# A fused graph-attention, feed-forward and expert kernel: dense sums from PSUM, nine result buffers, shorter first and last dispatches, three pairs a period over the last sixteen batches

## The chip, the cores and the metric

The kernel runs on one core of one Trainium2 chip. The metric is the device time of one execution in microseconds (us), the lower the better. A profile records one execution: its span runs from the first to the last instruction, and its own time lies a little above the span.

## The reference

Two layers follow one another on x, 64 batches of 256 nodes with 256 features, all in float32:

```python
x = x + gnn0(layernorm(x), adj)          # 4 heads of 64: leaky scores, masked softmax over nodes, elu
x = x + layernorm(x) @ ffn_w.T + ffn_b   # 256 -> 256
x = x + gnn1(layernorm(x), adj)          # 1 head of 256: leaky scores, masked softmax, relu
x = x + moe(layernorm(x))                # see below
```

In moe each of the 16,384 nodes is a token. The router gives 8 logits; the two largest, through a softmax over the two, are the token's weights. With e running over the 8 experts:

```python
h = gelu(tokens @ w1[e] + b1[e])
y = h @ w2[e] + b2[e]
out = tokens + sum over e of combine[:, e] * y      # combine is zero but for two experts
```

## The kernel before

**Batches.** One pass per batch of 256 nodes (two tiles of 128 rows) does both attention layers and the feed-forward layer: `batch_layers`. PE makes projections (L384, L419), scores (L454, L438) and attention sums (L475), DVE the masked scores z (L461, L443) and the statistics of the norms (L353, L354), ACT exponentials and copies out of PSUM, POOL the inverse deviations rstd (L361, L362). The normed result goes into a tile xng, its sum with the residual into `base`, which is stored to the output. Then PE makes the router logits into a tile lg.

**Routing and dispatch.** The first 62 batches are grouped in chunks: twelve of four batches, six of two, two of one. When a chunk is full, `route` finds each token's two experts and the place of each copy in a region per expert in DRAM, the buffer xs. POOL then sends the rows there with an indirect DMA (`send`, L877): two sends for each of the chunk's tiles of 128 rows, 248 in all.

**Pairs.** 256 rows of one expert's region are a pair; there are 131, of which 14 are a flush at the end, filled up with spare rows. `expert_pair` loads the pair's rows (xr, four DMAs of 64 KB, and xt, their numbers and weights) and the expert's first matrix (we, 288 KB) through SP, turns xr on DVE into sT (L116), makes the hidden layer on PE (ph, L783) and ACT (gelu, L789), the second product on PE (py, L798), adds the bias on DVE into a buffer y (L804), and scales y by the weights on ACT (L776). `scatter` then has POOL add y's rows to the output in DRAM with two indirect DMAs (L815). Because two pairs may hold rows of one token, each pair's scatters wait until those of the pair before have landed. The y buffers are a ring of `YBUFS` = 7; one is free again when its scatters have landed.

**Dense batches.** The last two batches are not routed. For each of them and each of 8 experts `dense_expert` uses the same `hidden` and `result`, and two DVE operations (L843) add w * y to `base`. So 16 of the 147 uses of y are dense ones.

**The order of the work.** One loop at the end of the kernel emits everything. Each job is a generator; in every step each active job advances to its next `yield`, in the order of the rank that it yielded last (a negative rank: once more in the same step). [...] Three steps are a period; the loop begins at step 2. A batch begins in every period at phase 2 (batch b at step 2 + 3b; batch 63 at 191, after which `more` becomes false). At phase 1 waiting pairs begin while there is `credit`: two are added each period, three when no batch is left to begin. At phase 2 up to two dense experts begin. One scatter begins in each step if one is waiting. A pair takes these steps, counted from its beginning: 0 loads of xr and xt; 1 load of we; 2 the turn (rank 95); 4 hidden; 5 result (rank 80); 6 scaling; its scatter from 7 on. `later(rank, phases)` makes a job wait for a phase; a chunk's sends go out two at a time, in two of the three phases.

Following the counters of this loop: the first pair begins at step 49, the eight of the second chunk at steps 61 to 70; the last pair at step 232; the last scatter is emitted at step 241.

Of the kernel before, what the change touches and what calls it, by code (L numbers as in the profile page):

```python
# [9 lines left out]
F32 = mybir.dt.float32  # L10
I32 = mybir.dt.int32
AF = mybir.ActivationFunctionType
ALU = mybir.AluOpType
AX = mybir.AxisListType

P = 128
# [11 lines left out]
def kernel(  # L28
# [17 lines left out]
    nc = tc.nc  # L46
    B, N, D = x.shape
    E = router.shape[0]
# [3 lines left out]
    NT = N // P  # L52
# [16 lines left out]
    ROW = D + 4  # L69
    TICKS = 3  # L70
# [3 lines left out]
    work = ctx.enter_context(tc.tile_pool(name="work", bufs=2))  # L74
    small = ctx.enter_context(tc.tile_pool(name="small", bufs=4))
# [171 lines left out]


    C_B1, WROW = KT * D, KT * D + 64
    WBUFS, XBUFS, YBUFS = 7, 5, 7  # L250
    wpack = tc.dram_tile([E, P, WROW], F32, name="wpack")
    w2s = const.tile([P, E, KT * D], F32, tag="w2s", name="w2s")
    b2s = const.tile([P, E, D], F32, tag="b2s", name="b2s")
# [158 lines left out]
    def projected1(xT, rstd, b):  # L412

        q = q1s[b % 2]
        pqs = []
        for t in range(NT):
            pq = bank("pq", [D + 3])
            for k in range(KT):
                nc.tensor.matmul(  # L419
                    pq, xT[:, k, t * P : (t + 1) * P], wx1[:, k, :],  # L420
                    start=(k == 0), stop=(k == KT - 1),
                )
            pqs.append(pq)
        ex = small.tile([P, NT, 3], F32, tag="ex1", name="ex1")
        for t, pq in enumerate(pqs):
            nc.scalar.activation(ex[:, t, :], pq[:, D:], AF.Exp, scale=rstd[:, t : t + 1])
            nc.scalar.activation(
                q[:, t, :D], pq[:, :D], AF.Copy, scale=rstd[:, t : t + 1]
            )
        me = work.tile([P, NT, N], F32, tag="me", name="me")  # L430
        for j in range(NT):
            nc.scalar.activation(me[:, j, :], masks[1][:, j, :], AF.Copy, scale=ex[:, j, 0:1])
        return q, ex, me
# [274 lines left out]
    GROUP = 8  # L708

    def expert_pair(j, n, ids, ef, regs, needs):  # L710

        i = j % GROUP
        upto = min(j + GROUP, n)
        if i == 0:
            _, regs["e"] = nc.values_load_multi_w_load_instructions(
                ids[0:1, 0, j:upto], engines=[mybir.EngineType.SP], min_val=0, max_val=E - 1,
                skip_runtime_bounds_check_because=WHY,
            )
            _, regs["t"] = nc.values_load_multi_w_load_instructions(
                ids[0:1, 1, j:upto], engines=[mybir.EngineType.SP], min_val=0, max_val=E * CAP,  # L720
                skip_runtime_bounds_check_because=WHY,
            )
        e_sp, t_sp = regs["e"][i], regs["t"][i]
        xr = io.tile([P, PAIR // S, KT * S], F32, tag="xr", name="xr", bufs=XBUFS)
        loads = [
            nc.sync.dma_start(
                out=xr[g * S : (g + 1) * S],
                in_=xs_d.rearrange("(t c q) f -> t q c f", c=PAIR // S, q=S)[
                    bass.ds(t_sp, 1), :, :, g * KT * S : (g + 1) * KT * S
                ].rearrange("t q c f -> (t q) c f"),  # L730
            )
            for g in range(P // S)
        ]

        xt = small.tile([P, 2, ROW - D], F32, tag="xt", name="xt", bufs=12)
        loads.append(
            nc.sync.dma_start(
                out=xt,
                in_=xs_d.rearrange("(t k p) c -> t p k c", p=P, k=2)[
                    bass.ds(t_sp, 1), :, :, D:  # L740
                ].rearrange("t p k c -> (t p) k c"),
            )
        )
        for load in loads:
            tc.add_to_no_dep_group("rows", load.ins)
            for name in needs:
                tc.add_manual_dep(
                    load.ins, name, AFTER, reason="any sent row may lie in the pair"
                )
        yield 90  # L750
        we = io.tile([P, WROW], F32, tag="we", name="we", bufs=WBUFS)
        nc.sync.dma_start(
            out=we, in_=wpack[bass.ds(e_sp, 1), :, :].rearrange("e p c -> (e p) c")
        )
        yield 95
        xT = turned(work.tile([P, KT, PAIR], F32, tag="sT", name="sT", bufs=3), xr)
        w = small.tile([P, 2], F32, tag="w", name="w", bufs=8)
        yield 30
        yield 30
        hT = hidden(xT, we)  # L760
        yield -65
        nc.vector.scalar_tensor_tensor(
            w[:, :, None], xt[:, :, 1:2], ef[:, j : j + 1], xt[:, :, 2:3],
            op0=ALU.is_equal, op1=ALU.mult,
        )
        nc.vector.tensor_tensor(w[:, :, None], w[:, :, None], xt[:, :, 3:4], ALU.add)
        yield 80
        if i == 0:
            _, regs["x"] = nc.values_load_multi_w_load_instructions(
                ids[0:1, 0, j:upto], engines=[mybir.EngineType.PE, mybir.EngineType.DVE],  # L770
                min_val=0, max_val=E - 1, skip_runtime_bounds_check_because=WHY,
            )
        y = result(hT, bass.ds(regs["x"][i], 1))
        yield 2
        for t in range(2):
            nc.scalar.activation(y[:, t, :], y[:, t, :], AF.Copy, scale=w[:, t : t + 1])  # L776
        scatters.append((y, xt))
# [13 lines left out]
            )  # L791
        return hT

    def result(hT, e):
        py = bank("py", [2, D])
        for t in range(2):
            for f in range(KT):
                nc.tensor.matmul(  # L798
                    py[:, t, :], hT[:, f, t * P : (t + 1) * P],
                    w2s[:, e, f * D : (f + 1) * D].rearrange("p e c -> p (e c)"),  # L800
                    start=(f == 0), stop=(f == KT - 1),
                )
        y = io.tile([P, 2, D], F32, tag="y", name="y", bufs=YBUFS)
        nc.vector.tensor_add(y, py, b2s[:, e, :].to_broadcast([P, 2, D]))  # L804
        return y
# [25 lines left out]
    def dense_expert(b, e):  # L831

        own = dense_batch[b]
        yield 90
        we = io.tile([P, WROW], F32, tag="we", name="we", bufs=WBUFS)
        nc.sync.dma_start(out=we, in_=wpack[e])
        yield 40
        yield 30
        hT = hidden(own["xT"], we)
        yield 80  # L840
        y = result(hT, slice(e, e + 1))
        for t in range(NT):
            nc.vector.scalar_tensor_tensor(  # L843
                own["base"][:, t, :], y[:, t, :], own["w"][:, t, e : e + 1],
                own["base"][:, t, :], op0=ALU.mult, op1=ALU.add,
            )
        if e == E - 1:
            while b == B - 1 and (scatters or len(added) < 2 * PAIRS):
                yield 99
            d = nc.sync.dma_start(  # L850
                out=out_rows[b * N : (b + 1) * N, :].rearrange("(t p) d -> p t d", p=P),
                in_=own["base"],
            )
            before = added[-2:] + based if b == B - 1 else []
            tc.declare_no_dep(
                d.ins, query=SYNC, group="out", keep=before,
                reason="no row is added to here, or every add is in their chain",
            )
            for ins in before:
                tc.add_manual_dep(d.ins, ins.name, AFTER, reason="filling rows were added here")  # L860
            tc.add_to_no_dep_group("out", d.ins)
            nc.sync.nop()
# [10 lines left out]
    order, order_steps = [], []  # L873
# [14 lines left out]
    def later(rank, *phases):  # L888

        yield rank  # L890
        while order_steps[-1] % TICKS not in phases:
            yield rank

    def route(c, row0, nt, n, last, xng, lg):
# [59 lines left out]
        for t in range(nt):  # L954
            for k in range(2):
                send(xng[t // NT][:, t % NT, :], pos[:, k, t : t + 1])
            if n and spread and t in (1, 3):
                ids, ef = next(parts) or (None, None)
            if not last:
                yield from later(95, 1, 2)  # L960
            elif t % 2:
                yield 95
# [53 lines left out]
    def jobs():  # L1016
        b = done = taken = 0
        for c, nb in enumerate(CHUNKS + (1,) * DENSE):
            nt = nb * NT
            lg = keep.tile([P, nt, E], F32, tag="lg", name=f"lg_{c}", bufs=10)  # L1020
            xng = []
            row0 = b * N
            done += nt
# [13 lines left out]

    batches = jobs()
    step, more, credit = 2, True, 0.0
    SETUP_AT = 3  # L1040
    with tc.manual_schedule():
        while more or active or waiting or dense_jobs or scatters:
# [6 lines left out]
            if step >= SETUP_AT and setup:  # L1049
                begin(setup.pop(0)(), 90)  # L1050
            if phase == 1:
                credit = min(credit + (2.0 if more else 3.0), 3.0)
                while waiting and credit >= 1.0:
                    credit -= 1.0
                    begin(waiting.pop(0)(), 90)
# [58 lines left out]
```

## Time and profile before

| | |
|---|---|
| median of three runs | 1666.84 us (1666.26 to 1670.07) |
| profiled execution, its own time | 1670.08 us |
| its span | 1668.3 us |
| mean granted TensorE clock | 0.958 |
| PE busy | 1495.5 us, 90% |
| DVE busy | 1317.4 us, 79% |
| ACT busy | 833.2 us, 50% |
| POOL busy | 889.4 us, 53% |
| scatters L815 | 262, mean 1591 ns of issue |
| sends L877 | 248, mean 1012 ns of issue |
| sums y, L804 | 147, mean 688 ns |
| multiply-adds into base, L843 | 32, mean 482 ns |
| from the last scatter's issue to the end of the span | 10.0 us |

PE is TensorE's matmuls, DVE VectorE, ACT ScalarE, POOL GpSimd, SP the engine that issues most DMAs. A group or a wait is named by line, engine and tile (out<-in). In a wait the left side is who waited and the right side whom it waited for, with the total, the number of times and the longest. The timeline gives the start, the duration, the engine, the line, the operation and, in brackets, how long the engine sat idle before it and what ended that. The number behind xN in a merged row counts instructions; one matmul of the program on float32 is two in the trace.

### The profile page before, as it was taken

How to read it: one execution, taken by the hardware profiler on the slowest of the kernel's cores; microseconds unless marked ns; L12 is line 12 of the kernel's file. 1: busy time of each engine (PE TensorE's matmuls, PEld its weight loads, DVE VectorE, ACT ScalarE, POOL GpSimd, SP SyncE). 2: the span in 40 equal slices, each digit the busy share in tenths (PEclk: the TensorE clock that was granted, in tenths of full speed). 3: DMA queues.
4: the chain of work that ended last, by engine and by line, in shares of the span. 5: the costliest groups of instructions: out<-in, count | busy, mean ns of one | idle time of the engine just before them, and what ended most of it. 6: DMA issues, size and time to landing. Idle time of an engine off the chain costs nothing.

```text
span 1668.3 us, 30242 instructions
## 1 busy us (share of the span) xinstructions
PE 1495.5 (90%) x8474; PEld 1311.2 (79%) x8474; DVE 1317.4 (79%) x4478; ACT 833.2 (50%) x1832; POOL 889.4 (53%) x853
## 2 busy tenths in 40 slices
PE   5898888899999999999999999999989987678782
PEld 4777777688888888888888888888878876567671
DVE  6888989999898988898989898998889876423330
ACT  0243444455656666666666665655555565323221
POOL 0121433545757575757575757574764666444344
PEclk8999999999999999999999999999999998879986
DMA  3812223255757575756575766665564676866753
GB/s 107 231 41 58 61 70 94 74 142 114 167 118 163 118 159 129 140 132 146 133 149 134 145 133 146 137 140 121 123 142 99 115 156 141 200 135 112 155 107 44
DMA packets 365285, 209.74 MB, mean 126 GB/s; under 512 B 264376, under 2 KB 335040, under 8 KB 365120
## 3 DMA queue, kind: packets, MB, share of 16 engines
q1 hardware_dynamic: 314496, 139.43, 34.0%
q0 software_dynamic: 49632, 67.39, 22.5%
q8 instruction: 70, 1.15, 0.3%
q10 hardware_dynamic: 992, 0.99, 0.2%
q14 instruction: 95, 0.78, 0.2%
HBM read 118.55 MB, written 89.15 MB: 124 GB/s over the span
## 4 chain that ended last, share of the span: by engine, by line
PE 55%; DVE 26%; DMA 6%; issue 5%; POOL 4%; ACT 2%; SPq 1%; DVEq 0%; POOLq 0%; ACTq 0%
PE ph L783 14%; PE pv L475 12%; PE py L798 9%; PE pq L384 5%; PE pq L419 4%; DVE z L461 4%; PE pf L529 4%; DVE stats L353 4%; DMA out_dram<-y,xt 3%; PE pt L368 3%; POOL out_dram L815 2%; DVE mv L354 2%; PE pl L599 2%; PE pd L454 1%; DVE x L535 1%
## 5 line engine op out<-in xcount | busy, mean ns | idle before, releaser
L815 POOL DMA_INDIRECT out_dram<-y,xt x262 | 416.7, 1591 | 255.4 <-DMA out_dram<-y,xt 73.0
L475 PE MATMUL pv<-q,z 128*128 128x65 f32 (+1 forms) x2560 | 369.8, 299 | 6.7 <-DVE z L461 5.3
L475 PEld LDWEIGHTS pv<-q,z 128*128 128x128 f32 x2560 | 331.9, 194 | 19.5 <-DVE z L461 5.8
L783 PE MATMUL ph<-sT,we 128*128 128x256 f32 x1048 | 259.1, 405 | 56.2 <-DVE sT L116 47.1
L361 POOL TENSOR_SCALAR rstd<-mv 128x4 f32<-128x4 f32 (+1 forms) x132 | 69.7, 528 | 436.1 <-DVE mv L354 352.9
L877 POOL DMA_INDIRECT xs<-xng,pos x248 | 251.1, 1012 | 69.2 <-issue 66.9
L783 PEld LDWEIGHTS ph<-sT,we 128*128 128x128 f32 x1048 | 209.8, 205 | 90.9 <-DVE sT L116 50.6
L798 PE MATMUL py<-w2s,hT 128*128 (+1 forms) x1176 | 263.9, 379 | 1.4 <-DVE z L461 0.7
L798 PEld LDWEIGHTS py<-w2s,hT 128*128 128x128 f32 x1176 | 219.7, 190 | 29.7 <-DVE z L461 1.0
L374 ACT COPY xT<-pt 128x512 f32<-128x512 f32 x192 | 113.3, 590 | 222.4 <-PE pt L368 184.7
L804 DVE TENSOR_TENSOR y<-py,b2s 128x512 f32<-128x512 f32 x147 | 97.5, 688 | 158.9 <-PE py L798 88.7
L789 ACT ACTIVATE hT<-ph,we 128x256 f32<-128x256 f32 x294 | 122.8, 471 | 183.3 <-PE ph L783 80.9
L461 DVE SCALAR_TENSOR_TENSOR z<-pd,q,mask 128x256 f32<-128x256 f32 x512 | 211.1, 473 | 0.3 <-PE pd L454 0.2
L362 POOL TENSOR_TENSOR rstd<-rstd,mhalf 128x4 f32<-128x4 f32 (+1 forms) x132 | 162.6, 1232 | 11.0
L776 ACT ACTIVATE y<-y,w 128x256 f32<-128x256 f32 x262 | 113.1, 501 | 104.4 <-DVE y L804 96.3
L353 DVE BATCH_NORM_STATS2 stats<-x 128x6 f32<-128x256 f32 x384 | 156.3, 407 | 2.2
L384 PE MATMUL pq<-wx,xT 128*128 128x268 f32 x512 | 137.9, 415 | 8.6 <-DVE wt L257 4.2
L419 PE MATMUL pq<-wx,xT 128*128 128x259 f32 x512 | 129.1, 394 | 15.5 <-ACT xT L374 11.2
L529 PE MATMUL pf<-wfT,xT 128*128 128x256 f32 x512 | 125.0, 388 | 0.0
L419 PEld LDWEIGHTS pq<-wx,xT 128*128 128x128 f32 x512 | 91.9, 189 | 41.9 <-ACT xT L374 22.4
L384 PEld LDWEIGHTS pq<-wx,xT 128*128 128x128 f32 x512 | 100.9, 202 | 30.1 <-issue 6.9
L551 ACT ACTIVATE rel<-pv,rinv 128x256 f32<-128x256 f32 x128 | 54.0, 474 | 108.2 <-DVE rinv L482 95.8
(151 smaller groups left out, 2233.8 us busy)
## 6 DMA issues: line engine op xcount, KB each, us to landing
we<-wpack SPq DMA_DIRECT2D x147, 288.0 KB
xr<-xs SPq DMA_DIRECT2D x524, 64.0 KB
xblk<-in_x_dram SPq DMA_DIRECT2D x256, 64.0 KB
xin<-in_x_dram SPq DMA_DIRECT2D x64, 256.0 KB
out_dram<-base SPq DMA_DIRECT2D x64, 256.0 KB
out_dram<-y,xt POOLq DMA_INDIRECT x262
xs<-xng,pos POOLq DMA_INDIRECT x248
xs<-fill SPq DMA_DIRECT2D x9, 260.0 KB
```

What stands on the lines that cost most here:

```text
L353: nc.vector.bn_stats(stats[:, t, :], src[:, t, :])
L362: nc.gpsimd.tensor_tensor(rstd[:, :n], rstd[:, :n], mhalf[:, :n], ALU.pow)
L384: nc.tensor.matmul(pq.rearrange("p h c -> p (h c)"), xT[:, k, t * P : (t + 1) * P], wx[:, k, :], start=(k == 0), stop=(k == KT - 1),)
L419: nc.tensor.matmul(pq, xT[:, k, t * P : (t + 1) * P], wx1[:, k, :], start=(k == 0), stop=(k == KT - 1),)
L461: nc.vector.scalar_tensor_tensor(z[:, j, :], pd[:, i, :], q[:, j, h, d + 2 : d + 3], mask[:, j, :], op0=ALU.max, op1=ALU.mult,)
L475: nc.tensor.matmul(pv[:, h, :], z[:, j, t * P : (t + 1) * P], q[:, j, h, : d + 1], start=(j == 0), stop=(j == NT - 1),)
L529: nc.tensor.matmul(pf[:, t, :], xT[:, k, t * P : (t + 1) * P], wfT[:, k, :], start=(k == 0), stop=(k == KT - 1),)
L783: nc.tensor.matmul(ph[:, f, :], we[:, k * D + f * P : k * D + (f + 1) * P], xT[:, k, :], start=(k == 0), stop=(k == KT - 1),)
L789: nc.scalar.activation(hT[:, f, :], ph[:, f, :], AF.Gelu, bias=we[:, C_B1 + f : C_B1 + f + 1])
L798: nc.tensor.matmul(py[:, t, :], hT[:, f, t * P : (t + 1) * P], w2s[:, e, f * D : (f + 1) * D].rearrange("p e c -> p (e c)"), start=(f == 0 ...
L815: d = nc.gpsimd.indirect_dma_start(out=out_rows, out_offset=bass.IndirectOffsetOnAxis(ap=xt[:, t, 0:1].bitcast(I32), axis=0), in_=y[:, t, ...
L877: d = nc.gpsimd.indirect_dma_start(out=xs_d[: E * CAP * PAIR, :], out_offset=bass.IndirectOffsetOnAxis(ap=at, axis=0), in_=xe, in_offset=None,
```

## The change

1. `WBUFS, XBUFS, YBUFS = 7, 5, 9`: the ring of y has nine buffers.
2. Dense experts no longer take a y. The product stays in PSUM, and four DVE operations per expert add w * py and w * b2 to `base`.
3. While the last sixteen batches are begun (from step 3 * 48 = 144 on), three pairs may begin in a period instead of two.
4. The first two chunks send four times in each step, in consecutive steps. Once no batch is left to begin, no job waits for a phase in `later`.
5. Once no batch is left to begin, a pair's turn is emitted at rank 75, that is ahead of the sums of the same step, instead of 95.
6. The dense batch's store is emitted one step later, with rank 99.
7. Buffers: me 2 to 1, xt 12 to 14, w 8 to 12, lg 10 to 7. The lists of expert numbers for PE and DVE are loaded once per group of eight under a key of the group, with unchanged contents and number of loads.

By the same counters, after the change the first pair begins at step 40, the eight of the second chunk at 52 to 61, the last pair at 229, and the last scatter is emitted at step 237. Pairs begun per period at steps 145, 148, 151, 154: three, two, two, one before; three, three, two, none after, and so on in each cycle of four batches up to step 178. At steps 184, 187, 190 and 193 three begin instead of two.

```diff
-    WBUFS, XBUFS, YBUFS = 7, 5, 7
+    WBUFS, XBUFS, YBUFS = 7, 5, 9
...
-        me = work.tile([P, NT, N], F32, tag="me", name="me")
+        me = work.tile([P, NT, N], F32, tag="me", name="me", bufs=1)
...
-        xt = small.tile([P, 2, ROW - D], F32, tag="xt", name="xt", bufs=12)
+        xt = small.tile([P, 2, ROW - D], F32, tag="xt", name="xt", bufs=14)
...
-        yield 95
+
+        yield 95 if more else 75
         xT = turned(work.tile([P, KT, PAIR], F32, tag="sT", name="sT", bufs=3), xr)
-        w = small.tile([P, 2], F32, tag="w", name="w", bufs=8)
+        w = small.tile([P, 2], F32, tag="w", name="w", bufs=12)
...
-    def result(hT, e):
+    def product(hT, e):
         py = bank("py", [2, D])
...
+        return py
+
+    def result(hT, e):
+        py = product(hT, e)
         y = io.tile([P, 2, D], F32, tag="y", name="y", bufs=YBUFS)
         nc.vector.tensor_add(y, py, b2s[:, e, :].to_broadcast([P, 2, D]))
         return y
...
-        y = result(hT, slice(e, e + 1))
-        for t in range(NT):
-            nc.vector.scalar_tensor_tensor(
-                own["base"][:, t, :], y[:, t, :], own["w"][:, t, e : e + 1],
-                own["base"][:, t, :], op0=ALU.mult, op1=ALU.add,
-            )
+        py = product(hT, slice(e, e + 1))
+        for t in range(NT):
+            for add in (py[:, t, :], b2s[:, e, :]):
+                nc.vector.scalar_tensor_tensor(
+                    own["base"][:, t, :], add, own["w"][:, t, e : e + 1],
+                    own["base"][:, t, :], op0=ALU.mult, op1=ALU.add,
+                )
         if e == E - 1:
+            yield 99
...
         yield rank
-        while order_steps[-1] % TICKS not in phases:
+        while more and order_steps[-1] % TICKS not in phases:
             yield rank
...
-            if not last:
+            if c < 2:
+                if t % 2:
+                    yield 95
+            elif not last:
                 yield from later(95, 1, 2)
...
-            lg = keep.tile([P, nt, E], F32, tag="lg", name=f"lg_{c}", bufs=10)
+            lg = keep.tile([P, nt, E], F32, tag="lg", name=f"lg_{c}", bufs=7)
...
+    DRAIN_AT = TICKS * (B - 16)
...
-                credit = min(credit + (2.0 if more else 3.0), 3.0)
+                credit = min(credit + (2.0 if step < DRAIN_AT else 3.0), 3.0)
```

More of the change, by code (lines that the diff above doesn't have):

```diff
@@ L712, in expert_pair @@
         i = j % GROUP
-        upto = min(j + GROUP, n)
+        upto = min(j - i + GROUP, n)
         if i == 0:
@@ L767, in expert_pair @@
         yield 80
-        if i == 0:
-            _, regs["x"] = nc.values_load_multi_w_load_instructions(
-                ids[0:1, 0, j:upto], engines=[mybir.EngineType.PE, mybir.EngineType.DVE],
+        if ("x", j - i) not in regs:
+            _, regs["x", j - i] = nc.values_load_multi_w_load_instructions(
+                ids[0:1, 0, j - i : upto], engines=[mybir.EngineType.PE, mybir.EngineType.DVE],
                 min_val=0, max_val=E - 1, skip_runtime_bounds_check_because=WHY,
             )
-        y = result(hT, bass.ds(regs["x"][i], 1))
+        y = result(hT, bass.ds(regs["x", j - i][i], 1))
         yield 2
```

## The prediction

> **What bounds the kernel now.** I read the slices first, to find stages with different limits, then busy time by stretch, then the waits and the timeline of the stage that looked unbound. Slices (page, part 2; each digit is a tenth of a 41.7 us slice):
>
> ```profile
> PE   5898888899999999999999999999989987678782
> DVE  6888989999898988898989898998889876423330
> POOL 0121433545757575757575757574764666444344
> DMA  3812223255757575756575766665564676866753
> ```
>
> PE is full up to about slice 31; then everything drops and nothing is full. Busy time by stretch says how full:
>
> ```profile
> core 0: us, PE busy (x) PEld busy (x) DVE busy (x) ACT busy (x) POOL busy (x), PEclk, DMA share, GB/s
> 778.00:864.00 86.00, 85.05 (x511) 76.14 (x510) 77.26 (x257) 52.74 (x113) 56.06 (x53) 1.00 0.66 141
> 1223.00:1293.00 70.00, 68.16 (x385) 60.53 (x385) 63.74 (x232) 40.35 (x87) 36.08 (x36) 0.95 0.51 111
> 1347.00:1410.00 63.00, 48.73 (x221) 41.81 (x220) 46.14 (x228) 32.64 (x69) 42.91 (x41) 0.88 0.73 153
> 1460.00:1557.00 97.00, 74.75 (x320) 63.66 (x320) 31.74 (x74) 27.67 (x64) 41.91 (x28) 0.90 0.68 133
> 1557.00:1636.00 79.00, 70.28 (x288) 59.31 (x288) 27.52 (x66) 25.09 (x58) 34.94 (x23) 0.90 0.62 111
> ```
>
> First row: four batches with eight pairs in steady state, PE 99% busy. The last batch is begun at 1293 us (its transpose of xblk). From 1460 the batches are gone; pairs, dense experts and scatters remain, and PE is busy 77%. What holds that stage, from the waits of 1460 to 1636 (us in total, times, longest):
>
> ```profile
> PE ph L783 <- DVE sT L116: 39.6, 8, 9.8
> DVE y L804 <- DMA out_dram<-y,xt: 19.4, 6, 6.2
> ```
>
> and one period of it in the timeline (start, us, engine, what, idle before and its releaser):
>
> ```profile
> 1480.13 0.69 DVE L804 TENSOR_TENSOR y<-py,b2s 128x512 f32<-128x512 f32 x1 [3.20 <-DMA out_dram<-y,xt]
> 1480.85 1.54 POOL L815 DMA_INDIRECT out_dram<-y,xt  x1 [3.79 <-DMA out_dram<-y,xt]
> 1486.65 0.69 DVE L804 TENSOR_TENSOR y<-py,b2s 128x512 f32<-128x512 f32 x1 [5.83 <-DMA out_dram<-y,xt]
> ...
> 1489.69 1.89 DVE L116 STREAM_TRANSPOSE sT<-xr 128x512 f32<-128x512 f32 x3
> 1490.45 2.07 PE L783 MATMUL ph<-sT,we 128*128 128x256 f32 x4 [9.07 <-DVE sT L116]
> ```
>
> All seven y buffers are out; the sum at L804 waits for a scatter to land; the three transposes of the next pairs stand behind it on DVE; PE waits for them. Last, the end, nothing but scatters:
>
> ```profile
> 1651.90 1.54 POOL L815 DMA_INDIRECT out_dram<-y,xt  x1 [2.97 <-DMA out_dram<-y,xt]
> 1653.75 1.54 POOL L815 DMA_INDIRECT out_dram<-y,xt  x1 [0.30 <-issue]
> 1658.29 1.54 POOL L815 DMA_INDIRECT out_dram<-y,xt  x1 [2.99 <-DMA out_dram<-y,xt]
> ```
>
> One pair's two scatters must land before the next pair's are issued: 6.4 us a pair here, with nothing else running. So there are two bounds: PE while batches run, the scatter chain at the end, and between them a loop that couples the two.
>
> [...] The chain of waits has 3.67 to 3.70 us from issue to landing at the end, of which 1.54 is the issue: 2.1 left[...].
>
> **The change, part by part.** Steps are those of the emitting loop, followed by hand through its counters; a batch enters every 3 steps (a period), a steady period is 21.45 us (85.8 for four), a step 7.15.
>
> (a) Three pairs a period from step 144. The queue of waiting pairs is fed two per batch. Up to step 180 it is empty at the end of each cycle of four batches before and after, so pairs only move inside a cycle: 3, 2, 2, 1 begun per period becomes 3, 3, 2, 0. From step 181 there is backlog: at 184, 187, 190 and 193 three are begun instead of two. From 194 both begin three. So four pairs go from the drain into periods that still hold batches. With the last dispatches (below) the last scatter is emitted at step 237 instead of 241.
>  Gain: four scatters fewer in the chain at the end. In the drain the spacings that the chain alone sets run from 6.4 to 7.2 us, about 6.9: 4 x 6.9 = -28.
>  Cost 1: a pair is 8 matmuls at L783 and 8 at L798, 222 ns apart in the drain (40 in 8.9 us): 16 x 0.222 = 3.55 us of PE. Steps 184 to 197 are PE-full (68.2 of 70): 4 x 3.55 = +14. If PE's later holes (14 us in 1347 to 1410) absorb it, 0.
>  Cost 2: a period with no pair holds 21.45 - 7.1 = 14.35 us of PE work, but DVE needs (77.3/4) - 2 x 1.75 = 15.8 there, and batches without pairs took 18 (277 to 350: 73 for four). So 1.4 to 3.7 us lost a cycle in PE-full time, three or four cycles: +4 to +14; +6 taken.
>
> (b) Nine y buffers, none for dense experts, and the turn at rank 75 once no batch is left to begin. Five y a period came from seven buffers; now three from nine. The turns stand ahead of the sums on DVE, so PE no longer waits 2.4 to 9.8 us a period. If xr came late, the sums and the scatters would now stand behind it; but in the drain before it is issued 14 to 41 us ahead of its turn, and SP's place in the order is not touched. [...] PE needs 5 experts x 3.55 = 17.7 us a period, the chain 3 x 6.9 = 20.7. The chain becomes the bound, against about 22 now (turns at 1490, 1512, 1532, 1557, 1579, 1600, 1623): 1.3 us x 8 periods = -10. Ends: 0 if the chain itself slows with more traffic, -20 if it runs at 6.4.
>
> (c) Dense sums from PSUM. Removed 16 sums of 688 ns, added 32 multiply-adds. [...] the trace shows 464 to 473 ns with a PSUM source (L535, L461) and 482 without (L843), so 0.48 us each: 32 x 0.48 - 16 x 0.69 = +4.3 us of DVE, 0.5 a period, under DVE's 70% idle time. 0; without that cover +4. The PSUM bank is held 1.9 us instead of 0.7; PE comes round to it half a period later.
>
> (d) First dispatches: chunks 0 and 1 issue four sends a step for four steps, instead of two in two steps of three; their nine pairs come nine steps sooner, but chunk 2's stay, so PE work is only swapped between two cycles: 0. POOL has 4 x 1.28 = 5.1 us of sends a step plus 1.33 norms x 1.76 = 2.3, in steps of 6: rstd may come late. 8 steps x 1.4 = +11 at worst; POOL waits for DVE's mv up to 10 us there, which hides most: +2. Nothing below 0 unless PE's 10 us of holes in 277 to 350 are used, -5.
>
> (e) Last dispatches: no waiting for phases once batches are out; the last send is at step 206 instead of 208, in (a)'s four steps. One buffer of me: written once a period, read a step later: 0. lg in 7, xt in 14, w in 12, the register lists, the dense store one step later (it now stands behind the loads on SP): 0; if SP's place matters, a few us either way.
>
> Sum: -28 + 14 + 6 - 10 + 0 + 2 = -16 on the span of 1668.3 (its run 1670.08): 1652. The median of the runs is 1666.84, so I forecast 1650 to 1651.
>
> **Rivals.**
>  *Absorbed* (0.22): PE's later holes take the four pairs, so cost 1 falls away, and the chain runs near 6.6: -28 - 16 + 6 + 2 = -36, 1631. For: 14 us of PE idle in 1347 to 1410, 16 in 1410 to 1460. Against: PE is 97% full just before.
>  *Chain slows* (0.15): the drain's DMA share is 0.62 to 0.83; with the same bytes in less time scatters land later, spacing 7.3, (b) gains nothing: -29 + 14 + 6 + 2 = -7, 1660. This is the change not doing what it says.
>  *POOL takes over* (0.13), slower: scatters now come one a step in runs of eight and, from step 188, without end, while batches still need rstd. POOL then has 3.7 (scatter) + 1.7 (sends) + 2.3 (norms) = 7.7 us a step against 7.15, and a scatter that waits for the one before holds rstd behind it: the trace has ACT L392 waiting 80 us for rstd in all. Against: POOL is 65% busy in steady state and the four steps without scatters catch up 3 us each. If not caught up, eight steps x 0.55 = 4.4 a cycle x 4, plus 15 steps x 0.8 = 30: +14, 1681. It decides from about 16 us of stretch over steps 152 to 203, 0.3 a step.
>
> **How the numbers follow.** Forecast 0.50, span of cases 1640 to 1660. The unknown costs (cost 1 from 0, cost 2 to 14, (b) from 0 to -20, (d) to 11) and the rivals reach from 1626 to beyond 1680; 1628 to 1667 leaves out the slow rival and some of the best case. A measurement here tells about 0.3% (5 us) from no change: faster is all of the forecast and of *absorbed* and half of *chain slows*, 0.80; same 0.08; slower 0.12.
>
> **What would show it.** Waits of y for out_dram and of ph for sT gone in the drain; scatters 6.6 to 7 us apart there without the 8 to 9 us hole per group of three; turns of the last pairs about 15 us earlier; steady stretches unchanged (86 us for four batches), the last batch's first transpose some 10 us later than 1293, since PE is fuller. Wrong if the holes remain, if scatters spread, or if ACT's waits for rstd grow between 1000 and 1400.

## The result and the profile after

The change makes the kernel slower: 1684.19 us in the median of five runs (1676.36 to 1687.07) against 1666.84; the ratio is 1.0101, with a 95% interval of 1.0081 to 1.0121. The forecast was 1650, and its range ended at 1667. The profiled execution has a span of 1684.0 us.

The slices of the page after the change, answering to the four shown of the kernel before:

```profile
PE   5898888899899999999999999898999997599840
DVE  5888988898998989898989898888988877544320
POOL 0121526157447575657575756467574677433444
DMA  3812223455456575656665665647474666896633
```

After a hole in slices 34 and 35, PE is now nearly full in 36 to 38, which are the drain, but the span is 16 us longer (a slice is 42.1 us here). Busy time by stretch after the change (same columns as before: start and end, length, PE, PEld, DVE, ACT and POOL busy with counts, PE clock, DMA share, GB/s):

```profile
778.00:864.00 86.00, 85.05 (x513) 76.15 (x511) 77.11 (x255) 52.62 (x113) 55.35 (x54) 1.00 0.65 140
1316.00:1374.00 58.00, 56.85 (x327) 50.66 (x327) 49.92 (x188) 36.75 (x80) 42.04 (x38) 1.00 0.65 132
1471.00:1540.00 69.00, 69.00 (x319) 60.66 (x319) 29.81 (x66) 27.69 (x63) 27.84 (x18) 0.99 0.82 171
1540.00:1610.00 70.00, 60.67 (x266) 51.67 (x264) 25.10 (x62) 19.95 (x50) 28.20 (x19) 0.95 0.61 120
```

The steady state is as it was. In the first part of the drain (1471 to 1540) PE is busy 69.0 of 69 us, so the stall that the prediction showed is gone. Waits of the drain, 1471 to 1622:

```profile
DVE y L809 <- DMA out_dram<-y,xt: 54.2, 10, 9.6
...
POOL out_dram L820 <- DMA out_dram<-y,xt: 33.8, 9, 7.1
```

No wait of ph for sT is left, but y waits for scatters longer than before (54.2 us against 19.4), with nine buffers instead of seven. The results that PE now gives sooner stand in a longer queue. The timeline shows the queue's head:

```profile
1525.93 1.54 POOL L820 DMA_INDIRECT out_dram<-y,xt  x1 [0.30 <-ACT hT L790]
...
1533.68 1.54 POOL L820 DMA_INDIRECT out_dram<-y,xt  x1 [6.21 <-DMA xr<-xs]
1535.53 1.54 POOL L820 DMA_INDIRECT out_dram<-y,xt  x1 [0.30 <-issue]
...
1539.47 0.69 DVE L809 TENSOR_TENSOR y<-py,b2s 128x512 f32<-128x512 f32 x1 [5.29 <-DMA out_dram<-y,xt]
1540.19 1.54 POOL L820 DMA_INDIRECT out_dram<-y,xt  x1 [3.12 <-DMA out_dram<-y,xt]
```

POOL sat idle 6.2 us between two pairs and 3.1 us between the next two, while y's stood ready (the last scaling of the y that is added at 1533.68 ended at 1485.0): the scatters are one chain, in which each pair waits for the landing of the one before.

Where the time went is read by laying the two traces side by side at equal steps of the emitting loop. Batch b's first transpose marks step 2 + 3b; later steps are marked by the scatters in their order (start of a pair's first scatter at L815 before, L820 after):

| point | before, us | after, us | after minus before |
|---|---|---|---|
| batch 12 | 205.0 | 208.0 | +3.0 |
| batch 16 | 277.0 | 285.3 | +8.3 |
| batch 24, first dispatches done | 434.5 | 446.3 | +11.8 |
| batch 48, three a period begins | 949.6 | 961.1 | +11.5 |
| batch 60, step 182 | 1222.8 | 1245.0 | +22.2 |
| scatter of step 191 | 1301 | 1325 | +24 |
| scatter of step 203 | 1379 (the 93rd pair's) | 1422 (the 97th pair's) | +43, four pairs ahead |
| last scatter | 1658 (step 241) | 1674 (step 237) | +16 |

So there are three losses of 12, 12 and 19 us and one gain of 27. These are single executions: at batch 8, ahead of any send, the traces of all runs below lie between 132.9 and 139.1 us, so a microsecond or two in the first rows says little.

### The profile page after: what moved, and what is told of

It reads as the page before. It is cut to its first block, busy times and chain, and to the rows that moved or that the text cites. A ratio compares the mean times of both kernels' runs of the same rounds, so it can differ in the third digit from the quotient of the medians.

```text
span 1684.0 us, 30247 instructions
## 1 busy us (share of the span) xinstructions
PE 1496.0 (89%) x8474; PEld 1313.9 (78%) x8474; DVE 1323.9 (79%) x4494; ACT 821.6 (49%) x1826; POOL 887.4 (53%) x853
## 4 chain that ended last, share of the span: by engine, by line
PE 59%; DVE 16%; DMA 9%; POOL 6%; issue 4%; ACT 4%; SPq 2%; POOLq 0%; DVEq 0%; ACTq 0%
PE pv L475 14%; PE ph L784 12%; PE py L799 11%; PE pq L384 6%; DMA out_dram<-y,xt 5%; PE pq L419 5%; PE pf L529 4%; PE pt L368 3%; POOL out_dram L820 3%; DVE z L461 3%; DVE stats L353 2%; PE pl L599 2%; ACT xT L374 2%; POOL xs L884 1%; SPq L726 1%
## 5 line engine op out<-in xcount | busy, mean ns | idle before, releaser
L820 POOL DMA_INDIRECT out_dram<-y,xt x262 | 416.0, 1588 | 256.6 <-DMA out_dram<-y,xt 78.6
L799 PE MATMUL py<-w2s,hT 128*128 (+1 forms) x1176 | 267.7, 384 | 9.9 <-DVE base L849 6.4
L784 PE MATMUL ph<-sT,we 128*128 128x256 f32 x1048 | 242.5, 387 | 11.3 <-DMA we<-wpack 9.1
L784 PEld LDWEIGHTS ph<-sT,we 128*128 128x128 f32 x1048 | 200.6, 195 | 39.0 <-issue 9.8
L809 DVE TENSOR_TENSOR y<-py,b2s 128x512 f32<-128x512 f32 x131 | 85.9, 686 | 92.7 <-DMA out_dram<-y,xt 57.9
L384 PE MATMUL pq<-wx,xT 128*128 128x268 f32 x512 | 144.5, 430 | 8.6 <-DVE wt L257 4.2
L384 PEld LDWEIGHTS pq<-wx,xT 128*128 128x128 f32 x512 | 104.5, 209 | 32.0 <-issue 7.2
L419 PEld LDWEIGHTS pq<-wx,xT 128*128 128x128 f32 x512 | 92.0, 190 | 42.3 <-ACT xT L374 31.0
L354 DVE BATCH_NORM_AGGREGATE mv<-stats 128x2 f32<-128x6 f32 x512 | 93.2, 182 | 17.5
```

The source lines that it names most:

```text
L384: nc.tensor.matmul(pq.rearrange("p h c -> p (h c)"), xT[:, k, t * P : (t + 1) * P], wx[:, k, :], start=(k == 0), stop=(k == KT - 1),)
L419: nc.tensor.matmul(pq, xT[:, k, t * P : (t + 1) * P], wx1[:, k, :], start=(k == 0), stop=(k == KT - 1),)
L784: nc.tensor.matmul(ph[:, f, :], we[:, k * D + f * P : k * D + (f + 1) * P], xT[:, k, :], start=(k == 0), stop=(k == KT - 1),)
L799: nc.tensor.matmul(py[:, t, :], hT[:, f, t * P : (t + 1) * P], w2s[:, e, f * D : (f + 1) * D].rearrange("p e c -> p (e c)"), start=(f == 0 ...
L820: d = nc.gpsimd.indirect_dma_start(out=out_rows, out_offset=bass.IndirectOffsetOnAxis(ap=xt[:, t, 0:1].bitcast(I32), axis=0), in_=y[:, t, ...
```

## The experiments

Theory A is what this table suggests: each loss belongs to the part of the change that acts at these steps. Theory B puts the loss into the drain. In the expectations, "the second kernel" and "the third kernel" are those of the second and third experiments; the third is the base of most later ones. Runs are compared through their ratios to the kernel before, run beside them on the same chip; 0.1% is 1.7 us. Intervals in brackets are of 95%.

**1. First sends put back.**

```diff
-            if c < 2:
-                if t % 2:
-                    yield 95
-            elif not last:
+            if not last:
```

> The changed kernel with the first two chunks' sends put back to two in two of three steps; all else as changed. Theory A (read from the two traces at equal steps: the changed kernel is 12 us behind once chunk 1's pairs are done, another 12 after steps 144 to 180, another 19 after steps 191 to 203, and then gains 27 by four scatters fewer): 12 us under the changed kernel, about 1672. Theory B (the loss comes from scatters that follow one another in every step of the drain and from the dense sums, and early differences are absorbed later): within 3 us of the changed kernel, 1681 to 1687.

1671.88 us, ratio 1.0010 (0.9999 to 1.0020).

**2. Three a period only from step 180.**

```diff
-    DRAIN_AT = TICKS * (B - 16)
+    DRAIN_AT = TICKS * (B - 4)
```

> The changed kernel with three pairs a period only from step 180 on, so that steps 144 to 179 begin 3, 2, 2, 1 pairs a period as before, while the four pairs of steps 184 to 193 are still drawn ahead. Theory A: the 12 us of steps 144 to 180 come back, about 1672. Theory B: within 3 us of the changed kernel. The prediction's own term for this part was 6 us, with 4 to 14 as its ends.

1669.99 us, ratio 0.9996 (0.9985 to 1.0008).

**3. Both of these edits.**

> Both of the two edits above together: what is left of the change is nine y buffers, dense sums from PSUM, the turn ahead of the sums, four pairs drawn ahead and the shorter last dispatches. Theory A: 1684 - 24 = 1660, about 7 us under the kernel before (0.4% faster). Theory B: above 1675.

1657.67 us, ratio 0.9925 (0.9911 to 0.9938): faster than both kernels.

**4. The first edit, and the pace of before.**

```diff
-                credit = min(credit + (2.0 if step < DRAIN_AT else 3.0), 3.0)
+                credit = min(credit + (2.0 if more else 3.0), 3.0)
```

> The changed kernel with the first sends back and the pace of pairs as before (two a period while batches are left to begin, then three): only buffers, dense sums, the turn's place, the store's place and the last dispatches are changed. Theory A: the scatter chain was already the bound of the drain before, at about 7.3 us a pair with loads running, and PE freed from waiting gives nothing: 1664 to 1670, no difference from before. The prediction's term for this part was -10: 1657. Theory B: above 1672.

1674.39 us, ratio 1.0028 (1.0013 to 1.0044).

The four close the account. In per cent of the time before: the first dispatches cost 0.71 to 0.91 (runs 2 and 3; changed kernel and run 1), 12 to 15 us. The pattern of steps 144 to 179 costs 0.85 to 1.05, 14 to 17 us. The four pairs drawn ahead gain 1.03 (runs 4 and 3), 17 us. What is left, buffers, dense sums, the turn's place and last dispatches, is +0.28, 5 us (2 to 7). Theory B is refuted: from the 97th pair's first scatter to the last pair's, run 3 takes 250.5 us and the changed kernel 252.0, and run 3 is the fastest so far. The +0.28 of run 4 was not expected; its profiled execution (span 1667.4), one of its fastest, shows no such loss, so it stays unexplained. Run 4 has all of (b), the prediction's central part, and TensorE waits for no sT in its drain, yet it is not faster than the kernel before.

**5 and 6. What sets the pace of the drain.** Run 5 leaves out the dense experts' work but keeps their loads; run 6 leaves out the loads too.

```diff
         we = io.tile([P, WROW], F32, tag="we", name="we", bufs=WBUFS)    # run 6: without these
         nc.sync.dma_start(out=we, in_=wpack[e])                          # two lines
...
-        hT = hidden(own["xT"], we)
         yield 80
-        py = product(hT, slice(e, e + 1))
-        for t in range(NT):
...
```

> The third kernel (both edits back) with the dense experts' hidden layer, product and sums left out, so that the last two batches miss their experts; their weight loads (288 KB each, two a period) stay. It takes 7.2 us of TensorE work out of each period of the drain and no transfer. Theory A (the chain of scatters sets the drain, and its pace is set by the loads beside it, not by waits for y): the spacing of scatters in the drain stays at 7.2 to 7.5 us a pair, the end moves by less than 5 us. Rival (the long gap once per group of three is a wait for the results, as the prediction read it): the gaps shrink, spacing 6.9 or less, the end 12 us earlier or more.

> As the run before, with the dense experts' weight loads left out as well: 0.58 of about 2 MB of loads a period are gone. Theory A: scatters land sooner, spacing 6.5 to 6.9 us a pair over some 24 pairs, the end 10 to 20 us earlier than with the loads. Rival: no difference from the run before.

1661.53 us, ratio 0.9957 (0.9943 to 0.9972), and 1652.41, 0.9899 (0.9882 to 0.9916). From the 103rd pair's scatter to the 121st's, the spacing in the traces is 7.69 us in run 3 (1446 to 1585), 7.70 in run 5 and 7.19 in run 6 (1447 to 1577); over the last ten pairs it is 6.4 in all three. Run 5 has 42 us less PE work than run 3 in this stretch and the same spacing of scatters; taking away transfers shortens it. Busy time of run 5, then of run 3:

```profile
1446.00:1585.00 139.00, 89.54 (x348) 72.69 (x347) 34.98 (x92) 35.35 (x85) 55.74 (x37) 0.83 0.72 148
```

```profile
1446.00:1585.00 139.00, 131.44 (x592) 114.43 (x590) 56.98 (x140) 49.96 (x116) 55.97 (x37) 0.96 0.73 151
```

So the chain's own pace under load is the bound, and TensorE's share is not. Two expectations were missed in size: the spacing of 7.7 in runs 3 and 5 is above the 7.2 to 7.5 named, and that of run 6 did not fall to 6.9 or less; the loads of three pairs a period remain there. By its ratio run 5 is also 0.32% (5 us) above run 3, though the two traces have the same span (1658.6); this is open.

**9 and 10. Waits in the drain.** The turn back behind the sums, and seven y buffers, each alone in the third kernel.

```diff
-        yield 95 if more else 75
+        yield 95
```

> The third kernel with the turn of xr back at rank 95, behind the sums of its step, to the end. Theory A (TensorE's waits in the drain cost nothing, since the chain of scatters is its bound): within 4 us of the third kernel, 1654 to 1662, with the waits of ph for sT back in the trace. The prediction's reading (these waits lengthen the period): 8 us or more over it.

```diff
-    WBUFS, XBUFS, YBUFS = 7, 5, 9
+    WBUFS, XBUFS, YBUFS = 7, 5, 7
```

> The third kernel with seven y buffers instead of nine. Theory A: within 4 us of the third kernel, 1654 to 1662: the sums wait longer, the scatters do not. If the scatters ever starve for a result: slower by 5 us or more.

1658.36 us, ratio 0.9906 (0.9876 to 0.9936), and 1660.01, 0.9917 (0.9887 to 0.9947): neither differs from the third kernel. The waits came as foreseen, first run 9, then run 10, 1446 to 1610:

```profile
PE ph L784 <- DVE sT L116: 19.2, 7, 2.7
```

```profile
DVE y L809 <- DMA out_dram<-y,xt: 81.2, 17, 7.7
```

In the third kernel there is none of the first and 45.9 us of the second. 19 us of TensorE waiting, or 35 us more of VectorE waiting, cost nothing that these runs can tell. With run 4, where the whole stall is gone without a gain, this makes the prediction's central stall a symptom.

**8. The pattern in all cycles.** `DRAIN_AT = 0` in the third kernel.

> The third kernel with three pairs a period allowed from the start, so that every cycle of four batches from chunk 1 on begins 3, 3, 2, 0 pairs instead of 3, 2, 2, 1: seven more full cycles than in the changed kernel, ten in all. If a period without pairs leaves TensorE short of work in each cycle: 12 us per three cycles, so about 40 us over the third kernel, 1690 to 1705. If the loss of steps 144 to 180 comes from something particular to these steps: under 1680.

1744.05 us, ratio 1.0438 (1.0419 to 1.0457): 86 us over the third kernel, twice what was expected, 95.7 us for four batches from batch 32 to 48 instead of 85.7. Its waits in 600 to 800:

```profile
ACT q L392 <- POOL rstd L362: 23.4, 4, 9.6
DVE q L400 <- ACT q L392: 17.9, 4, 7.0
...
PE pd L454 <- ACT q L392: 12.7, 2, 7.0
```

Twice in 200 us, about once a cycle, TensorE stands about 6 and 7 us for q, q for rstd, and rstd for POOL. POOL's timeline up to one such rstd, with the last DVE statistics (mv) that this rstd reads:

```profile
731.02 1.59 POOL L820 DMA_INDIRECT out_dram<-y,xt  x1 [0.30 <-ACT me L432]
732.91 0.99 POOL L884 DMA_INDIRECT xs<-xng,pos  x1 [0.30 <-issue]
...
733.69 0.18 DVE L354 BATCH_NORM_AGGREGATE mv<-stats 128x2 f32<-128x6 f32 x1
...
734.20 0.99 POOL L884 DMA_INDIRECT xs<-xng,pos  x1 [0.30 <-issue]
738.30 1.61 POOL L820 DMA_INDIRECT out_dram<-y,xt  x1 [3.11 <-DMA out_dram<-y,xt]
740.22 1.57 POOL L820 DMA_INDIRECT out_dram<-y,xt  x1 [0.30 <-issue]
741.23 0.84 POOL L361 TENSOR_SCALAR rstd<-mv 128x4 f32<-128x4 f32 x1
742.16 1.04 POOL L362 TENSOR_TENSOR rstd<-rstd,mhalf 128x4 f32<-128x4 f32 x1
```

The rstd at 741 begins 7.4 us after its statistics are complete. It stands behind sends and two pairs' scatters, of which the second waited 3.1 us for the first to land. In the third kernel, 600 to 1000, the latest begins 4.0 us after its statistics. No y waits for a buffer in this stretch, so the ring of y is not the cause. The period of that rstd:

```profile
727.00:752.00 25.00, 17.09 (x95) 14.95 (x95) 17.32 (x56) 10.26 (x24) 17.37 (x16) 0.86 0.80 172
```

25 us for a period in which neither PE nor DVE has more than 17.4 us of work.

**11 and 12. The same without the scatters before step 180**, with the pattern in all cycles and with the old one.

```diff
         y, xt = scatters.pop(0)
+        if order_steps[-1] < 180:
+            skipped.append(2)
+            return
```

> The kernel with 3, 2 2, 1 turned into 3, 3, 2, 0 in every cycle, with the scatters of all steps before 180 left out (their rows are missing in the output; pairs are computed in full). It is to be held against the next run, which leaves out the same scatters with the old pattern. With scatters the pattern costs 86 us. If scatters in a row keep POOL from the norms, and TensorE waits for these in the period without pairs: the cost falls to under 40 us. If the period without pairs is short of TensorE work by itself: it stays at 70 or more.

> The third kernel with the scatters of all steps before 180 left out (their rows are missing in the output). In steady state TensorE is 99% busy, so the period stays: both theories have the batches at 85 to 86 us for four and the end within 5 us of the third kernel.

1662.79 us, ratio 0.9946 (0.9918 to 0.9973), and 1656.39, 0.9896 (0.9856 to 0.9935). Four batches take 86.3 and 85.8 us in steady state. The pattern's cost falls from 86 to 6 to 8 us (give or take 8), and in both traces no rstd in 600 to 1000 begins more than 0.5 us after its statistics. So most of the cost needs the scatters, and the traces show the way it takes, through POOL's queue to rstd; it is not a lack of TensorE work in the period without pairs. Leaving out the scatters takes away their memory traffic as well, and no run parts that from POOL's queue. In the changed kernel the same path shows at a smaller size: from batch 48 to 60 ACT's waits for rstd at L392 are 20.4 us against 7.0 in the third kernel, the latest rstd begins 5.2 us after its statistics against 3.7, and TensorE waits 4.9 us for q against 0.7. That is less than half of the 11 us that its trace loses there; the rest is not traced to a wait.

**7. Quick first sends, pairs held to their old steps.** The second kernel, with

```diff
         needs = sent[mark:]
+        while c < 2 and order_steps[-1] < (46, 58)[c]:
+            yield 95
```

> The third kernel with the quick first sends (four a step), but the pairs of these two chunks begin in their old steps (49, and 61 to 70), not nine steps sooner. It parts the two halves of the quick first sends, which together cost 12 us. If the sends crowd POOL and hold up the norms (the prediction's term, 2 us with 11 as its bad end): 7 us or more over the third kernel, 1665 to 1670. If moving the pairs into a cycle that had none is what costs: within 3 us of the third kernel, 1655 to 1661.

1655.70 us, ratio 0.9937 (0.9914 to 0.9959): no different from the third kernel (0.12% above it, give or take 0.26). Four sends in a step show no cost by themselves. The 12 us come with the pairs that are brought forward.

**13 and 14. Without the first nine scatters**, in the second and in the third kernel; the edit is that of run 11 with step 72 and 78.

> The second kernel (quick first sends and pairs nine steps sooner, old pattern) with the scatters of the first nine pairs left out (their rows are missing in the output). With these scatters it is 12 us slower than the third kernel. If they stand between the sends of the next chunk and hold up the norms on POOL: 8 us or more of the 12 come back, 1657 to 1663. If it is the pairs' own work on TensorE and VectorE in a stage that was not full: 1667 or more.

> The third kernel with the scatters of the first nine pairs left out, as the measure for the run before. Both readings: within 4 us of the third kernel, 1654 to 1662.

1658.00 us, ratio 0.9935 (0.9916 to 0.9955), and 1650.97, 0.9886 (0.9866 to 0.9906). The first looks like the scatters' reading, but its measure went down too, by 0.39% (6.5 us) where 4 us were allowed. Between the two, 0.49% (8 us, give or take 5) of the 0.71% remain. The traces put it lower: counted from batch 8, the second kernel is 10.0 us behind the third at batch 24 and 10.1 at batch 28; without the nine scatters in both, 7.1 and 3.6. So the scatters are a part of this loss and the pairs' own place another, and the shares are not settled.

## Why the prediction was wrong

**(b), the drain's period: wrong, 10 us.** The step that failed is "the spacings that the chain alone sets run from 6.4 to 7.2 us, about 6.9", with its "22 now". It counted the long gap in each group of three, 8 to 9 us, as a wait for new results. In the trace before, one of these long gaps ends as follows (timeline of the kernel before; the first line is the scaling of the y that the scatter at 1569.67 adds):

```profile
1545.87 0.91 ACT L776 ACTIVATE y<-y,w 128x256 f32<-128x256 f32 x2 [0.88 <-DVE y L804]
...
1569.67 1.54 POOL L815 DMA_INDIRECT out_dram<-y,xt  x1 [4.88 <-ACT hT L789]
1570.56 0.69 DVE L804 TENSOR_TENSOR y<-py,b2s 128x512 f32<-128x512 f32 x1 [10.95 <-PE py L798]
```

The scatter at 1569.67 comes ahead of the group's first sum at 1570.56 and adds a y that had been ready for 22.9 us. It had not waited for a result; what was left to wait for was the landing of the pair before. So it is throughout: of the 39 pairs from step 203 to the end before, none had its y ready less than 9.7 us ahead of its first scatter. The chain was already the only bound, at 7.3 us a pair (279 us for 38 steps of the chain), and runs 4, 5, 9 and 10 show that freeing TensorE, or letting it wait, moves nothing, while run 6 shows that fewer loads shorten the chain. The rival *chain slows* had this term as zero with the chain slowed down to 7.3; in the main it had been there before. It was right in a smaller part: for the same pairs, the 97th to the last, the chain took 246.0 us before, 247.4 in run 4, 250.5 in run 3 and 252.0 in the changed kernel, with 171 GB/s in 1471 to 1540 against 117 before.

**(a), four pairs ahead: right in sign, about right in size.** Predicted -28 + 14 = -14. Run 3 is 17 us under run 4, of whose time 5 us are unexplained, and 12.5 us under the kernel before. In the two traces both terms are larger, 27 for the gain and 19 for the cost, which leaves 8. "Steps 184 to 197 are PE-full (68.2 of 70)" read too much into its row, which ends at step 191; but PE is busy 56.9 of 58 us in 1316 to 1374 after the change, as the cost's reason wants. The 5 us above 4 x 3.55 were not parted.

**(a), cost 2: size and mechanism wrong.** Taken as 6 us, from TensorE short of work in a period without pairs. It was 14 to 17, and of the 86 us in run 8 about 79 go with the scatters. The right mechanism stood among the rivals as *POOL takes over*, with "4.4 a cycle" for the stretch; it came to about 4 to 6 a cycle in the changed kernel (three cycles) and 8.6 in run 8 (ten). The prediction held against it that POOL is 65% busy. That share counts no time in which POOL waits for a landing with rstd queued behind (3.1 us ahead of the scatter at 738.30 in run 8). A better reading was at hand in the trace before: once a cycle, behind the fourth of five scatters in consecutive steps, rstd begins 4.0 us after its statistics (680.97 against 676.98), at a place where TensorE does not yet wait for it. The change made the run of five one of eight, and in run 8 the 4.0 became 7.4. That this rival's 1681 lies near the measured 1684 is luck: it put 12 of its 30 us on fifteen steps from 188 on, which no run tests, and kept -10 for (b) and +2 for (d).

**(d), first dispatches: wrong, 12 to 15 us for 2.** "PE work is only swapped between two cycles: 0" failed. Its bad end of 11 us was put on the sends, which show no cost by themselves (run 7); the loss comes with the pairs that begin sooner. How it divides between these pairs' work and their scatters stays open (runs 13 and 14).

**(c), dense sums: the price was right; no run tests its zero alone.** In the changed kernel the multiply-adds take 478 ns (median of 32) with the PSUM source and 485 without, close to the 0.48 us each that the prediction took. PE waits 6.4 us for these sums in 1471 to 1622 (two waits of py for base), a wait that the prediction ruled out; PE is not the bound there. **(e):** run 4 leaves at most 0.44% for everything small, (b) and (c) included.

**Signs named beforehand.** The waits of ph for sT vanished and steady stretches stayed at 86 us, as said. The last turn came 31 us earlier (1593.3 against 1624.0), twice the 15 forecast, and the end did not follow. The waits of y for the scatters, forecast to go, grew. All three signs of being wrong came: the long gaps between scatters remain, the scatters did not move to 6.6 to 7 us but spread from 7.4 to 7.7 (103rd to 121st pair), and ACT's waits for rstd at L392 between 1000 and 1400 grew from 9.2 to 25.3 us. The last batch's first transpose came at 1316.5, 23 us later instead of 10.

**The range.** It let the unknown costs vary one at a time. With cost 2 at 14, (d) at 11 and (b) at 0 together, the prediction's own terms give -28 + 14 + 14 + 11 = +11, or 1679; that sum is for the span, which measured 1684. A common cause, that the work is brought closer together than POOL's queue (rstd up to 7.4 us behind its statistics in run 8) and the scatter chain (7.4 us a pair before, 7.7 after, 103rd to 121st pair) allow, is shown for cost 2 and (b), and for (d) only in part.

## What to carry to other kernels

Before a stalled engine is freed, look for what it waits for, and test whether that resource is a chain already working at its own pace under load: here a long gap in the chain (4.9 us of POOL idle ahead of a scatter whose y had been ready for 22.9 us; 7.1 us after the change at 1557.64, ended by a landing) was a slow landing, not a missing input, and removing TensorE's waits (39.6 us in 1460 to 1636) did not bring the end forward. How long each input had been ready tells the two apart. POOL's busy share said little here, as its queue held scatters that waited for landings: in 727 to 752 of run 8 it is busy 17.4 of 25 us, and rstd is 7.4 us behind its statistics. For such an engine look at how far it falls behind in the longest run of such work, and at who waits for the next thing in that queue. Work moved toward the start (12 to 15 us here) or bunched into fewer periods (14 to 17) is not free because the sum stays equal; the version that beat both kernels (run 3, 0.9925) gives up the first dispatches and the bunched pattern; of what it keeps, only the four pairs drawn ahead show a gain.

## What the runs showed of the hardware

A pair's two scatters of 128 rows each, where the next pair must wait for their landing, take 6.3 to 6.7 us a pair with nothing else running (after the change from 1648 to 1674, PE, DVE and ACT busy 0 us, 41 GB/s), 6.4 us over the last ten pairs of runs 3, 5 and 6, 7.2 us with the pairs' loads (run 6, 128 GB/s in that stretch), and 7.7 us with the dense loads as well (runs 3 and 5, 148 to 151 GB/s). A stall of 7 us on TensorE goes with a granted clock of 0.86 for its period (run 8, 727 to 752), against 1.00 in the next one (752 to 777). Work emitted behind an instruction that waited began after it: before the change the turns at 1489.69 behind the sum at 1486.65, which had waited 5.83 us for a landing, and in run 8 the rstd at 741.23 behind the scatter at 738.30, which had waited 3.1 us.
